# Where GpSimd's product pairs, the silu and softplus passes and y's sums stand in the order of a two-layer attention and state-space kernel

## The chip, the cores and the metric

The kernel runs on one core of one Trainium2 chip. The metric is the device time of one execution in microseconds; the time given for a kernel is the median over its runs. Shorter is better.

## What is computed

The input x has the shape (2, 256, 256, 128), f32. Two layers follow each other, each added to its own input after a group normalisation. The first is a row attention (q, k, v1, v2 and output projections of 128 channels). The second, in which the change lies, is a selective scan over the tokens of each image:

```python
xz = x @ in_proj_w.T;  xi, z = split(xz)              # 2 x 256 channels
xi = silu(depthwise_conv3x3(xi) + conv_b)              # xs
dts, Bs, Cs = split(x_proj_w @ xs)                     # 8, 16, 16 rows
delta = softplus(dt_w @ dts + dt_b)
h = exp(delta * A) * h + (delta * xs) * Bs             # per token, 256 x 16 states
y = sum_over_16_states(h * Cs) + Ds * xs
y = layernorm(y) * silu(z)
out = x + y @ out_proj_w.T
```

## The kernel before, in words

The first layer runs call by call until about 2670 us of the span; the rest is the second layer. That is cut into 128 steps (2 images x 64) of four image rows, T = 1024 tokens each. The 256 channels x 16 states of a step are 32 units of 128 partitions (32 channels x 4 states) by 1024 tokens. `unit(t)` (line 912 on) gives for unit t the step k, the half h of the channels (16 units each), the group m of four states and the quarter q of the half's channels. Four consecutive units share m, so their products sum into the same rows of y.

The order of all compute engines is written out by hand: under `tc.manual_schedule` a loop over slots t (lines 1051 to 1081) issues, once per unit, the instructions of that slot, and each engine executes its own in that order. What a slot holds for unit t:

- `drive` (line 960, instruction at 966): GpSimd multiplies delta\*x by B for a pair of units, 128 x 2048. Its buffer `hb` has room for three pairs. A pair is driven three slots ahead.
- `decay` (line 952, instruction at 956): ScalarE writes exp(delta\*A) of unit t+1 to PSUM, `da0` or `da1`, one buffer each for even and odd units.
- `scan` (978): VectorE runs the recurrence along the 1024 tokens.
- the product with C: either `product` (992), VectorE, one unit of 1024, right after its scan; or, for units in the list `POOLED`, `products` (1001), GpSimd, both units of the pair at once, two slots after the first of them. For these the scan writes to `hb` in place of PSUM. `POOLED` names the first unit of each pair; five pairs of sixteen are GpSimd's. The products lie in `yc`, which has room for four pairs.
- `add_up` (1024): eight TensorE matmul instructions (x16 in the profile) sum four units' products over the states into `y`, in PSUM, which has one buffer. They free two pairs of `yc`. `start_up` (1015) begins a new y with Ds\*xs every 16 units; `y_out` (1037) is ScalarE's copy of a finished y to SBUF, in slots 3 and 19, ahead of that slot's other pieces.
- `remember` (983): ScalarE keeps the last column of h as the next step's start.

Between these stand the pieces that prepare later steps and finish earlier ones. `project(k)` begins 72 slots ahead of step k: `turn` (658) and `normalise` (663) bring in rows, `conv` (676) is nine taps of matmuls for each half of channels and of tokens, `gate` (702) computes z, `states` (726) and `size` (744) compute B, C and delta. Their results all pass through one PSUM bank, the pool `ps_p`, so each piece waits until ScalarE has copied the one before it, one slot later (`conv_out` 687, `gate_out` 713, `states_out` 739, `size_out` 755). Three passes of ScalarE over a whole step, each between two loads of its function table, are `silu_z` (718), `silu_xs` (695) and `softplus` (763). `times` (773) forms delta\*x on GpSimd. `finish(k)` works off one row per eight slots: TensorE turns y (`turn`, 828), ScalarE sums squares (`stats`, 840), scales (`scales`, 846 and 848) and normalises (`norm`, 852), TensorE turns back (`back`, 863), VectorE multiplies by the silu of z (`gated`, 871), TensorE mixes (`mix`, 875 and 879), ScalarE copies out (`leave`, 889). Its PSUM pool `ps_f` has one bank.

Seen within a step of 32 slots, the pieces fall in four octaves of the same pattern: `turn` and three small pieces of `project` in the first four slots, then the nine taps of a conv over four slots, `back` in the second of these, `mix` in the last:

| slots | small pieces through the bank | conv taps | finishing row |
|---|---|---|---|
| 0 to 7 | states 0, 1; size at 2 | 3 to 6 | turn 0, back 4, mix 7 |
| 8 to 15 | size at 8, 9, 10 | 11 to 14 | turn 8, back 12, mix 15 |
| 16 to 23 | gate at 16, 17, 18 | 19 to 22 | turn 16, back 20, mix 23 |
| 24 to 31 | turn at 24, 25; gate at 26 | 27 to 30 | turn 24, back 28, mix 31 |

`start_up` stands in slots 5 and 21. `others` of a slot (everything but TensorE's pieces) are issued ahead of `on_pe` (TensorE's).

## Time and profile before

| | before |
|---|---|
| median of 3 runs | 16394.46 us (16359.25 to 16439.24) |
| span of the profiled run | 16364.8 us |
| mean granted TensorE clock | 0.917 |
| scan, VectorE | x4096, 2346 ns (to PSUM), 2338 ns (to SBUF) |
| product, VectorE, one unit | x2816, 1225 ns |
| pair of products, GpSimd | x640, 4531 ns |
| drive of a pair, GpSimd | x2048, 4543 ns |
| decay, ScalarE | x4096, 1122 ns |

A profile row of instruction groups names line, engine, operation, output and inputs, count, then busy time and the mean of one in ns, then the idle time of the engine just ahead of them with what ended most of it. A timeline row has start (us from the span's start), duration, engine, line and operation; in brackets stands the idle time ahead of it and what released it. Rows of consecutive like instructions are merged (x16). The answer on stretches has for each stretch its length, the busy time of PE, PEld, DVE, ACT and POOL with counts, then the granted TensorE clock as a share of full speed, the busy share of the DMA engines and GB/s. The waits view gives, for an engine's line and what it waited for, the total in us, how often, and the longest. In these rows DVE is VectorE, ACT ScalarE, POOL GpSimd, PE TensorE.

### The profile page before, as it was taken

The numbers are of one execution on the slowest core, as the hardware profiler recorded it, in microseconds if no ns is written. First come the engines' busy times: TensorE is split into PE (matmuls) and PEld (weight loads), VectorE is DVE, ScalarE is ACT, GpSimd is POOL, SyncE is SP. The second block draws the span as 40 slices with busy tenths as digits, with TensorE's granted clock in tenths as the row PEclk, the third lists the DMA queues.
The fourth block names the chain that finished last, engine by engine and source line by source line (L and its number), as shares of the span: only waits on it lengthen the run. The fifth ranks groups of instructions, "written<-read, shape, count | busy, mean of one in ns | idle before, by whom it ended". The sixth has DMA issues, their size and how long they took to land. (4 is left out here: it accounts for less than half of the span.)

```text
span 16364.8 us, 178796 instructions
## 1 busy us (share of the span) xinstructions
PE 14102.2 (86%) x59451; PEld 7209.7 (44%) x59451; DVE 14625.1 (89%) x12484; ACT 10765.1 (66%) x20003; POOL 13046.0 (80%) x3216
## 2 busy tenths in 40 slices
PE   6999997888888888888888888888888888888886
PEld 5877883333333333333333333333333333333333
DVE  7665555999999999999999999999999999999998
ACT  3555554666666666676666666666666666666665
POOL 0111114999999999999999899999999999999997
PEclk9999998899999898998999889898999898989998
DMA  4322224666666666666666666666666666666665
GB/s 184 133 88 81 90 80 144 237 230 236 234 239 231 227 237 229 233 241 232 226 238 232 227 231 231 233 230 233 239 235 235 229 234 232 233 235 230 232 237 178
DMA packets 1428913, 3452.17 MB, mean 211 GB/s; under 512 B 119784, under 2 KB 711184, under 8 KB 1407504
## 3 DMA queue, kind: packets, MB, share of 16 engines
q1 hardware_dynamic: 1427984, 3440.73, 59.7%
q8 instruction: 467, 7.65, 0.2%
q14 instruction: 462, 3.78, 0.1%
HBM read 2752.41 MB, written 687.88 MB: 210 GB/s over the span
## 5 line engine op out<-in xcount | busy, mean ns | idle before, releaser
L966 POOL TENSOR_TENSOR hb<-du_r,bb 128x2048 f32<-128x2048 f32 x2048 | 9255.6, 4543 | 555.4 <-DVE da L978 489.1
L978 DVE TENSOR_TENSOR_SCAN da<-da,state,hb 128x1024 f32<-128x1024 f32 x2816 | 6606.1, 2346 | 141.9 <-ACT da L956 139.7
L676 PE MATMUL u_ps<-xn,w_tap 128*128 128x512 f32 x9216 | 5005.0, 691 | 718.1 <-ACT sz L713 433.9
L956 ACT ACTIVATE da<-delta_r,a_neg 128x1024 f32<-128x1024 f32 x4096 | 4595.3, 1122 | 92.8 <-ACT state L983 2.2
L992 DVE TENSOR_TENSOR yc<-da,cc 128x1024 f32<-128x1024 f32 x2816 | 3449.1, 1225 | 487.1 <-PE y L1024 326.8
L676 PEld LDWEIGHTS u_ps<-xn,w_tap 128*128 128x128 f32 x9216 | 1941.9, 221 | 3379.7 <-issue 2273.1
L1001 POOL TENSOR_TENSOR yc<-hb,cc 128x2048 f32<-128x2048 f32 x640 | 2900.0, 4531 | 365.6 <-DVE hb L978 249.3
L978 DVE TENSOR_TENSOR_SCAN hb<-da,state,hb 128x1024 f32<-128x1024 f32 x1280 | 2960.0, 2338 | 114.2 <-ACT da L956 114.2
L983 ACT COPY state<-da 128x1 f32<-128x1 f32 x2816 | 454.0, 161 | 2857.2 <-DVE yc L992 2852.4
L1024 PE MATMUL y<-yc,sel 128*32 128x512 f32 x16384 | 2191.9, 654 | 18.0 <-POOL yc L1001 18.0
L435 POOL TENSOR_TENSOR x1g<-xc,bo_all 128x512 f32<-128x512 f32 x256 | 315.7, 1271 | 1843.8 <-DVE stats L484 1842.8
L828 PE MATMUL yt<-centre,ys 128*128 128x256 f32 x4096 | 1034.4, 396 | 471.1 <-ACT ob L889 471.1
L385 ACT ACTIVATE e<-s_ps,nmx 128x256 f32<-128x256 f32 x1024 | 478.6, 477 | 968.5 <-DVE nmx L376 952.4
L1024 PEld LDWEIGHTS y<-yc,sel 128*32 128x32 f32 x16384 | 451.9, 114 | 1475.6 <-issue 1221.9
L828 PEld LDWEIGHTS yt<-centre,ys 128*128 128x128 f32 x4096 | 744.2, 191 | 651.9 <-ACT ob L889 568.5
L744 PE MATMUL dt_ps<-xd,w_dt 8*128 8x512 f32 x1024 | 646.8, 715 | 322.8 <-ACT delta L755 139.7
L702 PE MATMUL z_ps<-xn,w_z 128*128 128x512 f32 x1024 | 569.6, 638 | 411.2 <-ACT sz L713 249.7
L879 PE MATMUL o_ps<-w_out,szr 128*128 128x128 f32 x4096 | 798.0, 277 | 0.0
L879 PE MATMUL o_ps<-w_out,yg 128*128 128x128 f32 x4096 | 797.3, 277 | 0.0
L889 ACT COPY ob<-o_ps 128x256 f32<-128x256 f32 x512 | 189.3, 370 | 860.8 <-PE o_ps L879 827.7
L352 DVE TENSOR_TENSOR v<-v_ps,bv_all 128x512 f32<-128x512 f32 x256 | 177.1, 692 | 593.1 <-PE v_ps L345 593.1
L879 PEld LDWEIGHTS o_ps<-w_out,yg 128*128 128x128 f32 x4096 | 668.5, 194 | 27.6
(133 smaller groups left out, 16988.4 us busy)
## 6 DMA issues: line engine op xcount, KB each, us to landing
bb<-bc_d SPq DMA_DIRECT2D x1024, 512.0 KB, 4.5
cc<-bc_d SPq DMA_DIRECT2D x1024, 512.0 KB, 4.5
delta_r<-delta_d SPq DMA_DIRECT2D x1024, 512.0 KB, 6.1
du_r<-du_d SPq DMA_DIRECT2D x1024, 512.0 KB, 5.5
sz_d<-sz SPq DMA_DIRECT2D x128, 1024.0 KB, 6.6
szr<-sz_d SPq DMA_DIRECT2D x512, 256.0 KB, 5.8
xs_d<-xs SPq DMA_DIRECT2D x128, 1024.0 KB, 6.7
xr<-xs_d SPq DMA_DIRECT2D x256, 512.0 KB, 5.3
```

What stands on the lines that cost most here:

```text
L385: nc.scalar.activation(e[:, i, :], o["s", r][:, i, :], AF.Exp, bias=o["nmx", r][:, i : i + 1], scale=SM, accum_out=o["den"][:, r, i : i + 1],)
L676: nc.tensor.matmul(o["u"], w_tap[:, h, tap, :], xn[:, i * RB + dy : i * RB + dy + RB, dx : dx + W], start=(tap == 0), stop=(tap == 8),)
L702: nc.tensor.matmul(o["z"], w_z[:, h, :], xn[:, 1 + i * RB : 1 + (i + 1) * RB, 1 : W + 1], start=True, stop=True,)
L744: nc.tensor.matmul(o["dt"], w_dt[:, h, :], o["xd"][0:DR, i * TB : (i + 1) * TB], start=True, stop=True,)
L828: nc.tensor.matmul(o["yt"][:, j, :], ys[k, h][:, t0 + j * P : t0 + (j + 1) * P], centre[:, (1 - h) * P : (1 - h) * P + DI], start=(h == 0) ...
L879: nc.tensor.matmul(o["o"][:, j, :], o[by][:, h, j * P : (j + 1) * P], w_out[:, i, h, :], start=False, stop=(j == WT - 1 and h == NH - 1 an ...
L956: nc.scalar.activation(da, spreads["delta", k, h, q], AF.Exp, scale=a_neg[:, g, m : m + 1])
L966: nc.gpsimd.tensor_tensor(hb, spreads["pair", k, h, q], repeats["bb", k, h, m].unsqueeze(1).to_broadcast([P, 2, T]), ALU.mult,)
L978: nc.vector.tensor_tensor_scan(u["h"], u["da"], u["hb"], st, ALU.mult, ALU.add)
L992: nc.vector.tensor_tensor(u["yc"], u["h"], repeats["cc", k, h, m], ALU.mult)
L1001: nc.gpsimd.tensor_tensor(yc, hb, repeats["cc", k, h, m].unsqueeze(1).to_broadcast([P, 2, T]), ALU.mult)
L1024: nc.tensor.matmul(y[q * CQ : (q + 1) * CQ, cols], sel, units[t + q]["yc"][:, cols], start=False, stop=(m == NSG - 1),)
```

## The change

Four things change, all of them in what stands where in the hand-written order; no instruction is added or taken away.

- `POOLED`: GpSimd's five pairs of products are those of units 6, 14, 22, 30, which end each eight scans, and 26; they were those of 2, 6, 10, 18 and 26.
- `silu_z`, `silu_xs` and `softplus` move up by one slot, from slots 21, 29 and 13 of a step to 20, 28 and 12: with the pairs of units 22, 30 and 14 now GpSimd's, the passes stand a slot further from those pairs' decays.
- `gated`, the product with silu of z on VectorE, moves up by one slot, from 6, 14, 22 and 30 to 5, 13, 21 and 29, ahead of those pairs' scans.
- `add_up` is always issued at the end of the slot two after its last unit, behind all TensorE pieces of that slot. Before, this held only where the second pair of the four units was GpSimd's; otherwise the sums stood a slot earlier, ahead of the slot's TensorE pieces. It was so for the groups of units 12 to 15, 20 to 23 and 28 to 31, whose sums stood in slots 17, 25 and 1 (of the next step) and now stand at the end of 18, 26 and 2.

```diff
@@ -587,7 +587,7 @@
-    POOLED = (2, 6, 10, 18, 26)
+    POOLED = (6, 14, 22, 26, 30)
@@ -790,15 +790,15 @@
-        at(base + 29, silu_z)
-        at(base + 37, silu_xs)
+        at(base + 28, silu_z)
+        at(base + 36, silu_xs)
...
-        at(base + 53, softplus)
+        at(base + 52, softplus)
@@ -899,7 +899,7 @@
             (2, scales),
             (3, norm),
             (4, back),
-            (6, gated),
+            (5, gated),
             (7, mix),
             (8, leave),
@@ -1070,13 +1070,11 @@
             for piece, args in others:
                 piece(*args)
-            if 0 <= t - 5 < end and (t - 5) % NQ == 0 and not pooled(t - 2):
-                add_up(t - 5)
             for piece, args in on_pe:
                 piece(*args)
             if 0 <= t - 5 < end and (t - 5) % NM == 0:
                 start_up(t - 5)
-            if 0 <= t - 6 < end and (t - 6) % NQ == 0 and pooled(t - 3):
+            if 0 <= t - 6 < end and (t - 6) % NQ == 0:
                 add_up(t - 6)
             if 0 <= t < end:
                 remember(t)
```

## The prediction

> **What bounds the kernel now.** First the page: engine totals and groups.

> ```profile
> PE 14102.2 (86%) x59451; PEld 7209.7 (44%) x59451; DVE 14625.1 (89%) x12484; ACT 10765.1 (66%) x20003; POOL 13046.0 (80%) x3216
> L978 DVE TENSOR_TENSOR_SCAN da<-da,state,hb 128x1024 f32<-128x1024 f32 x2816 | 6606.1, 2346 | 141.9 <-ACT da L956 139.7
> L992 DVE TENSOR_TENSOR yc<-da,cc 128x1024 f32<-128x1024 f32 x2816 | 3449.1, 1225 | 487.1 <-PE y L1024 326.8
> L1001 POOL TENSOR_TENSOR yc<-hb,cc 128x2048 f32<-128x2048 f32 x640 | 2900.0, 4531 | 365.6 <-DVE hb L978 249.3
> ```

> The state memsets (line 1056) start at 2670.9 and 9496.8 us, 64 steps apart: 106.65 us per step, 128 steps, 83% of the span. VectorE (DVE) sets the pace. In one ordinary step (unit 0 scans at 8626.47 us, the next step's at +105.75) it pauses three times; its waits between 4000 and 9000 us, and those three in the timeline:

> ```profile
> DVE yc L992 <- PE y L1024: 117.6, 94, 2.4
> DVE hb L978 <- ACT da L956: 38.3, 47, 0.8
> ```

> ```profile
> 8653.56 1.23 DVE L992 TENSOR_TENSOR yc<-da,cc 128x1024 f32<-128x1024 f32 x1 [0.96 <-PE y L1024]
> 8661.41 2.35 DVE L978 TENSOR_TENSOR_SCAN hb<-da,state,hb 128x1024 f32<-128x1024 f32 x1 [0.81 <-ACT da L956]
> 8667.02 1.23 DVE L992 TENSOR_TENSOR yc<-da,cc 128x1024 f32<-128x1024 f32 x1 [1.01 <-PE y L1024]
> ```

> They are units 8, 11 and 12 of the 32. Without them the step is 105.75 - 2.78 = 102.97 us; over the mean step DVE therefore loses 106.65 - 102.97 = 3.7 us, 471 us in 128 steps. That is all the change can win on DVE. Why is TensorE (PE) late with y's sums? The same step on PE, then its granted clock in stretches (PEclk is the third column from the end):

> ```profile
> 8660.23 1.12 PE L744 MATMUL dt_ps<-xd,w_dt 8*128 8x512 f32 x2 [0.78 <-ACT state L983]
> 8662.46 1.12 PE L744 MATMUL dt_ps<-xd,w_dt 8*128 8x512 f32 x2 [1.12 <-ACT delta L755]
> 8663.51 3.49 PE L1024 MATMUL y<-yc,sel 128*32 128x512 f32 x16
> ...
> 8683.97 1.92 PE L1024 MATMUL y<-yc,sel 128*32 128x512 f32 x16
> ...
> 8688.92 1.13 PE L702 MATMUL z_ps<-xn,w_z 128*128 128x512 f32 x2 [1.97 <-ACT sz L713]
> 8692.30 5.49 PE L676 MATMUL u_ps<-xn,w_tap 128*128 128x512 f32 x6 [2.26 <-ACT sz L713]
> ```

> ```profile
> 8660.25:8663.66 3.41, 2.29 (x8) 0.71 (x12) 2.60 (x2) 3.37 (x7) 3.41 (x2) 1.00 0.36 138
> 8663.66:8667.10 3.44, 3.44 (x17) 0.61 (x12) 2.43 (x3) 2.29 (x5) 3.44 (x2) 0.51 0.80 291
> 8687.50:8690.92 3.42, 1.13 (x2) 0.30 (x2) 3.42 (x2) 3.37 (x7) 3.42 (x2) 1.00 1.07 394
> 8690.92:8697.80 6.88, 5.50 (x8) 2.28 (x9) 6.75 (x5) 5.49 (x10) 6.80 (x3) 0.51 0.60 224
> ```

> One set of sums takes 1.92 us at full clock and 3.49 at half. Half clock follows a stretch of 3.41 us in which PE was busy 2.29 us or less, which is where it trades one PSUM bank with ScalarE (ACT) piece by piece: slots 0-3, 8-11, 16-19, 24-27. Last, ACT around slot 19, where y leaves PSUM (line 1037), and the silu pass in slot 21:

> ```profile
> 8688.30 0.57 ACT L713 COPY sz<-z_ps 128x512 f32<-128x512 f32 x1
> ...
> 8690.03 1.00 ACT L1037 COPY ys<-y 128x1024 f32<-128x1024 f32 x1
> ...
> 8696.02 1.28 ACT L718 ACT_TABLE_LOAD   x1
> 8697.31 1.91 ACT L718 ACTIVATE sz<-sz 128x2048 f32<-128x2048 f32 x1
> 8699.24 1.28 ACT L619 ACT_TABLE_LOAD   x1
> ```

> y_out waits for nothing here: its sums ran at 8683.97, ahead of the slot's piece. A pass with its two table loads occupies ACT for 4.5 us.

> [...]

> **The change, part by part.** Time runs from unit 0's scan. Unit lengths from the step above: 3.55 us with DVE's product, 2.25 without, plus 0.60 for each of four gate products.

> *The pairs.* Five before, five after; 10 x 2.25 + 22 x 3.55 + 4 x 0.60 = 103.0 either way: no DVE or POOL work is saved. What moves is where DVE runs fast. Before, units 2, 3, 6, 7 and 10 shorten the stretch in which PE has the dt pieces, nine taps and y's start: from scan 3 (9.4) to product 8's turn (26.1) are 16.7 us. After, 10.65 to 28.85: 18.2. PE's stretch from the first tap to the end of the sums was 13.38 to 26.98, 13.6 us, and begins about 4.6 us after scan 3: 28.85. The wait at 8 shrinks from 1 us to some 0.35 (nought if warm, 1.4 if PE comes late). The waits at 11 and 12 go: no pair lies at 10. POOL keeps up (a drive takes 4.5 us, a pair of products 4.5, a delta product 2.35, and a drive needs the buffer of three pairs before): drive 18 starts at 46.6 behind scan 13; with the first delta product after it, pair 14's products run from 53.4 to 57.9, the second to 60.3, drives 20, 22, 24, 26 to 78.4, products 22 from scan 23's end at 79.3 to 83.8, drives 28 and 30 to 92.9, products 26 to 97.4, drive 32 to 102.0. Scans 20, 28 and 32 are due at 67.0, 90.9 and 103.0: no wait for POOL, with 1.0 us to spare at the least.

> *Gate products up a slot.* Four of 0.67 us, as many as before. They ask for the transposes back at 21.3, 47.7, 74.3 and about 101; these end at 20.0, 45.1, 72.6 to 75.2, and about 100. The third can be late by 0.9, but scan 22 is then waiting for ACT anyway (below). Cost 0.

> *Softplus (slot 12) and silu of xs (28).* 4.5 us of ACT each. Softplus ends at 46.55, decay 14 at 47.9, scan 14 is at 48.3: hidden behind scans 12 and 13 and their products. Silu of xs likewise hides behind units 28 and 29. Cost 0.

> *The sums behind the pieces.* Sets that were ahead (slots 1, 17, 25) now stand after the piece of slots 2, 18, 26. This adds waits. Slot 18: gate piece starts when ACT has copied the previous one, scan 18 (59.9) + 2.42 = 62.3. Without the early sums PE is busy from 54.7 to 57.5, then only from 59.3 to 60.35: any 3.41 us window ending between 58.5 and 61.9 leaves it at half clock. So piece 2.0 (twice 1.0, to 64.35) and sums 1.9 to 3.7, taken as 2.85 since a busy window may end in them: they end at about 67.2 (65.3 if both are warm, 68.0 at worst). y_out, formerly free at scan 19 + 1.5 = 64.9, waits until then. Behind it in ACT's queue stand y_out, norm, gate copy (2.1 together, as traced): 69.35, then decay 21 to 70.6 (scan 21 at 70.55: 0.1 lost).

> *Silu of z in slot 20* comes next in that queue: 70.6 + 4.5 = 75.1, remember and decay 22 to 76.4. Scan 22 is due at 74.75: 1.65 us lost (0 to 2.6).

> *Octave 24 to 31.* With 22 and 26 pooled DVE is fast where PE does taps, y's start, mix, and the turns. The taps start at 69.4; nine taps of 0.89, transposes 0.44, y's start 1.72, sums 1.85 and 1.7 for one cold window end at 83.1; product 24 asks at 83.4: mean loss 0.2. Mix (2.3) ends at 85.4, leave 85.7, conv copy and xn copy 86.75, decay 26 88.05, stats 89.05, normalise 89.75, decay 27 91.05, against a scan due at 90.35: 0.7, the old wait at unit 11 (0.81) again. Slot 26: the second normalise (scales 0.4, normalise 0.65 after decay 27) lets the gate piece start at 92.15; PE had only two turns of 0.55 since 87.6, so it is cold: piece 2.0, sums 2.8 (1.9 to 3.7): 97.0. Product 28 asks at 93.3 + 2.45 = 95.75: 1.3 (0.3 to 2.1).

> Sum: 0.35 + 0.1 + 1.65 + 0.2 + 0.7 + 1.3 = 4.3 us per step in place of 3.7: +0.6 x 128 = +77 us. At the very end the last pair is POOL's 4.53 us instead of a DVE product: +4. 16394 + 81 = 16475 us.

> **Rivals.** *Forecast (0.46): the three waits move, two of them onto cold sums; slightly slower,* 16475. For it: a cold 3.49 us set is already in the trace exactly where one stands behind such a piece. *Faster (0.26): PE stays warm* behind the pieces, so y_out and product 28 don't wait: 4.3 - 1.65 - 1.3 = 1.3 us, -2.4 x 128 = -307: about 16090. For it: pairs now lie mostly where ACT and PE don't trade a bank. Against it: 1.05 us of work in a 3.4 us window is less than what went cold before. *Slower by much (0.13): lateness is handed on:* 22 at 2.6, 27 at 0.75, 28 at 2.0, 8 at 1.4, in all 6.75, +3.05 x 128 = +390: about 16785. For it: the chain mix, leave, turn, stats has no slack after unit 24. *No change (0.15):* waits at 22 and 28 just replace those at 8 and 12, 16395.

> **How the numbers follow.** The loss per step has its centre at 4.3, only just past the 0.5% bound (82 us, 0.64 us per step): of the forecast about 0.33 lies above it, 0.08 within and 0.05 below. Slower 0.33 + 0.13 = 0.46; same 0.08 + 0.14 = 0.22; faster 0.26 + 0.05 + 0.01 = 0.32. The range takes in the forecast's cold bounds (losses 2.5 to 6.4) and part of the faster case: 16170 to 16740.

> **What would show it.** Right: DVE waits for ACT at unit 22 of about 1.65 us and for PE at unit 28 of about 1.3; none at 11 or 12; y_out with a wait of about 2 us on PE; sums in slots 18 and 26 at 2.9 to 3.5 us; mean granted clock in the steps near 0.89 instead of 0.92. Wrong: sums of 1.92 us there with few DVE waits (faster), a DVE wait on POOL (pairs or drives late, which I put at zero), or waits at unit 8 above 1 us (slower by much).

## The result and the profile after

The changed kernel takes 16291.85 us (median of 4 runs, 16285.8 to 16300.5) against 16388.42 us before (median of 4; one run more than in the table above): ratio 0.9938, 95% interval 0.9913 to 0.9964. It is 0.6% faster, where 0.5% slower was forecast.

Engine totals and the groups that answer to those shown of before, from the page of the changed kernel:

```profile
PE 13879.5 (85%) x59451; PEld 7046.9 (43%) x59451; DVE 14642.8 (90%) x12484; ACT 10842.9 (67%) x20003; POOL 13035.7 (80%) x3216
L978 DVE TENSOR_TENSOR_SCAN da<-da,state,hb 128x1024 f32<-128x1024 f32 x2816 | 6607.2, 2346 | 163.1 <-ACT da L956 160.2
L992 DVE TENSOR_TENSOR yc<-da,cc 128x1024 f32<-128x1024 f32 x2816 | 3449.1, 1225 | 287.3 <-PE y L1024 113.8
L1001 POOL TENSOR_TENSOR yc<-hb,cc 128x2048 f32<-128x2048 f32 x640 | 2908.7, 4545 | 527.6 <-ACT state L983 493.0
```

The work is the same to the instruction. The idle time ahead of VectorE's products has gone from 487 to 287 us. The state memsets start at 2675.1 and 9471.4 us, so a step takes 106.19 us on average where it took 106.65. Both means take in one long step at the change of images, 121.27 us before and 120.88 after; without it the steps average 106.44 and 105.86 us. So some 0.2 of the 3.7 us that the prediction counted as the old loss per step is this one step.

In the first image most steps take about 105.81 us. VectorE's waits between 4000 and 9000 us (line waited at, total, times, longest), and the same waits in one such step, which starts at 7550.13 us:

```profile
DVE hb L978 <- ACT state L983: 80.0, 82, 1.7
DVE yc L992 <- PE y L1024: 14.8, 16, 2.2
DVE hb L978 <- ACT da L956: 8.5, 39, 0.2
```

```profile
7626.58 4.59 DVE L978 TENSOR_TENSOR_SCAN hb<-da,state,hb 128x1024 f32<-128x1024 f32 x2 [1.44 <-ACT state L983]
7640.94 2.35 DVE L978 TENSOR_TENSOR_SCAN hb<-da,state,hb 128x1024 f32<-128x1024 f32 x1 [0.22 <-ACT da L956]
7651.43 4.59 DVE L978 TENSOR_TENSOR_SCAN hb<-da,state,hb 128x1024 f32<-128x1024 f32 x2 [0.42 <-ACT state L983]
```

These are units 22, 27 and 30: in such a step the waits for TensorE at units 8 and 12 are gone, and the large wait is now for ScalarE. The second image looks different. From about 10300 to 14600 us steps of 106.10 and 105.53 us alternate. The waits between 10000 and 15000 us, then those of one long step (from 11906.32 us: units 21, 22, 28) and of the short one after it (from 12012.42 us: units 8, 12, 28):

```profile
DVE yc L992 <- PE y L1024: 69.8, 90, 1.4
DVE hb L978 <- ACT state L983: 41.8, 27, 1.7
DVE da L978 <- ACT da L956: 18.7, 22, 0.9
```

```profile
11977.86 2.36 DVE L978 TENSOR_TENSOR_SCAN da<-da,state,hb 128x1024 f32<-128x1024 f32 x1 [0.85 <-ACT da L956]
11983.78 4.59 DVE L978 TENSOR_TENSOR_SCAN hb<-da,state,hb 128x1024 f32<-128x1024 f32 x2 [1.71 <-ACT state L983]
12002.65 1.23 DVE L992 TENSOR_TENSOR yc<-da,cc 128x1024 f32<-128x1024 f32 x1 [0.44 <-PE y L1024]
...
12042.01 1.23 DVE L992 TENSOR_TENSOR yc<-da,cc 128x1024 f32<-128x1024 f32 x1 [0.86 <-PE y L1024]
12056.59 1.23 DVE L992 TENSOR_TENSOR yc<-da,cc 128x1024 f32<-128x1024 f32 x1 [0.41 <-PE y L1024]
12108.18 1.23 DVE L992 TENSOR_TENSOR yc<-da,cc 128x1024 f32<-128x1024 f32 x1 [1.42 <-PE y L1024]
```

So product 28 waits for TensorE in all of these, and the wait at unit 22 is in every second step only. Back to the step from 7550.13 us: ScalarE's timeline shows the cause of its wait at unit 22, y_out waiting for the late sums, with the silu pass right behind:

```profile
7617.17 1.01 ACT L1037 COPY ys<-y 128x1024 f32<-128x1024 f32 x1 [2.11 <-PE y L1024]
...
7619.50 1.12 ACT L956 ACTIVATE da<-delta_r,a_neg 128x1024 f32<-128x1024 f32 x1
7620.64 1.28 ACT L718 ACT_TABLE_LOAD   x1
7621.94 1.91 ACT L718 ACTIVATE sz<-sz 128x2048 f32<-128x2048 f32 x1
7623.87 1.28 ACT L619 ACT_TABLE_LOAD   x1
...
7625.35 1.12 ACT L956 ACTIVATE da<-delta_r,a_neg 128x1024 f32<-128x1024 f32 x1
```

In the same step, TensorE's timeline at slots 18 and 26, and the granted clock (third column from the end) in stretches of about 3.41 us:

```profile
7612.45 1.95 PE L702 MATMUL z_ps<-xn,w_z 128*128 128x512 f32 x2 [2.09 <-ACT sz L713]
7614.33 2.74 PE L1024 MATMUL y<-yc,sel 128*32 128x512 f32 x16
...
7642.08 1.13 PE L702 MATMUL z_ps<-xn,w_z 128*128 128x512 f32 x2 [1.67 <-ACT xn L663]
7643.14 1.92 PE L1024 MATMUL y<-yc,sel 128*32 128x512 f32 x16
```

```profile
7585.40:7588.87 3.47, 2.36 (x8) 0.69 (x12) 3.37 (x3) 3.41 (x7) 3.47 (x2) 0.98 0.53 171
7588.87:7592.28 3.41, 3.41 (x17) 0.56 (x10) 3.38 (x3) 2.56 (x6) 3.41 (x2) 0.52 0.95 294
...
7636.66:7640.07 3.41, 2.10 (x14) 1.66 (x13) 3.26 (x3) 3.35 (x10) 3.41 (x1) 1.00 0.63 192
7640.07:7643.48 3.41, 1.74 (x10) 0.56 (x11) 3.19 (x3) 3.38 (x8) 3.41 (x2) 1.00 0.43 141
```

Slot 18's sums ran partly at half clock, as forecast (2.74 us). Slot 26's ran at full clock (1.92), though TensorE was busy for only 2.10 and 1.74 us in the two stretches up to them; yet 2.36 us in the stretch of slots 9 and 10 were followed by half clock (granted 0.52, and the sums of slot 10 took 3.61 us). And 105.81 us are 31 times 3.413 us, as 106.10 + 105.53 = 211.63 us are 62 times; 3.413 us is the spacing of the granted clock's changes, measured below. These two facts are what the experiments are about.

### The profile page after: what moved, and what is told of

Read it like the earlier page. It is cut to its first block, busy times and chain, and to the rows that moved or that the text cites. A ratio compares the mean times of both kernels' runs of the same rounds, so it can differ in the third digit from the quotient of the medians.

```text
span 16298.5 us, 178168 instructions
## 1 busy us (share of the span) xinstructions
PE 13879.5 (85%) x59451; PEld 7046.9 (43%) x59451; DVE 14642.8 (90%) x12484; ACT 10842.9 (67%) x20003; POOL 13035.7 (80%) x3216
## 5 line engine op out<-in xcount | busy, mean ns | idle before, releaser
L978 DVE TENSOR_TENSOR_SCAN da<-da,state,hb 128x1024 f32<-128x1024 f32 x2816 | 6607.2, 2346 | 163.1 <-ACT da L956 160.2
L676 PE MATMUL u_ps<-xn,w_tap 128*128 128x512 f32 x9216 | 4481.8, 629 | 617.0 <-ACT state L983 607.5
L956 ACT ACTIVATE da<-delta_r,a_neg 128x1024 f32<-128x1024 f32 x4096 | 4588.5, 1120 | 91.8 <-ACT state L983 0.4
L992 DVE TENSOR_TENSOR yc<-da,cc 128x1024 f32<-128x1024 f32 x2816 | 3449.1, 1225 | 287.3 <-PE y L1024 113.8
L1001 POOL TENSOR_TENSOR yc<-hb,cc 128x2048 f32<-128x2048 f32 x640 | 2908.7, 4545 | 527.6 <-ACT state L983 493.0
L978 DVE TENSOR_TENSOR_SCAN hb<-da,state,hb 128x1024 f32<-128x1024 f32 x1280 | 2941.9, 2336 | 199.1 <-ACT state L983 166.4
L676 PEld LDWEIGHTS u_ps<-xn,w_tap 128*128 128x128 f32 x9216 | 1762.1, 201 | 3108.4 <-issue 2110.6
L1024 PE MATMUL y<-yc,sel 128*32 128x512 f32 x16384 | 2409.3, 712 | 16.6 <-POOL yc L1001 16.6
L983 ACT COPY state<-da 128x1 f32<-128x1 f32 x2816 | 458.2, 163 | 1266.7 <-DVE yc L992 1262.4
L1024 PEld LDWEIGHTS y<-yc,sel 128*32 128x32 f32 x16384 | 477.4, 121 | 1743.3 <-issue 1518.6
L702 PE MATMUL z_ps<-xn,w_z 128*128 128x512 f32 x1024 | 691.8, 763 | 628.2 <-ACT sz L713 389.6
L983 ACT COPY state<-hb 128x1 f32<-128x1 f32 x1280 | 247.0, 193 | 1262.2 <-DVE hb L978 1262.2
L744 PE MATMUL dt_ps<-xd,w_dt 8*128 8x512 f32 x1024 | 611.7, 678 | 345.2 <-ACT state L983 193.7
```

Source lines behind the costliest of these rows:

```text
L676: nc.tensor.matmul(o["u"], w_tap[:, h, tap, :], xn[:, i * RB + dy : i * RB + dy + RB, dx : dx + W], start=(tap == 0), stop=(tap == 8),)
L702: nc.tensor.matmul(o["z"], w_z[:, h, :], xn[:, 1 + i * RB : 1 + (i + 1) * RB, 1 : W + 1], start=True, stop=True,)
L744: nc.tensor.matmul(o["dt"], w_dt[:, h, :], o["xd"][0:DR, i * TB : (i + 1) * TB], start=True, stop=True,)
L956: nc.scalar.activation(da, spreads["delta", k, h, q], AF.Exp, scale=a_neg[:, g, m : m + 1])
L978: nc.vector.tensor_tensor_scan(u["h"], u["da"], u["hb"], st, ALU.mult, ALU.add)
L983: nc.scalar.copy(st, units[t]["h"][:, T - 1 : T])
```

## The experiments

Two theories were set against each other. SUM: each wait of VectorE adds to the step (the prediction's way of counting). LOCK: a step is drawn to a whole number of TensorE's clock windows, because a window's place in the step decides how late the sums are. The windows are read from the traces: in the second layer every one of the 1058 falls and rises of the granted clock in before, and of the 931 in after, lies on one grid of 3.4133 us, to 0.011 us, through steps of different length. A window is the stretch between two points of that grid, and 105.81 / 31 = 3.413 agrees. Mean step below is the distance of the two state memsets over 64 and so takes in the change of images. The last column has the step, or the repeating group of steps, that is most frequent among all 127. Ratios are to the kernel before on the same chip.

| kernel | us, median | ratio, 95% interval | mean step | most frequent step or group |
|---|---|---|---|---|
| before | 16388 | | 106.65 | 105.74 |
| after | 16292 | 0.9938 [0.9913, 0.9964] | 106.19 | 105.81; 105.53 and 106.10 in turn |
| before_late | 17134 | 1.0472 [1.0455, 1.0489] | 112.68 | 112.64 |
| after_passes | 16688 | 1.0201 [1.0186, 1.0216] | 109.28 | 109.44 |
| after_gates | 16339 | 0.9987 [0.9980, 0.9995] | 106.37 | 105.81 |
| after_sum17 | 16169 | 0.9883 [0.9868, 0.9898] | 105.22 | 104.40, 103.45, 106.18 in turn |
| after_pad | 16383 | 1.0011 [1.0005, 1.0018] | 106.99 | none |
| after_sum17_25 | 16281 | 0.9958 [0.9944, 0.9972] | 105.95 | 105.81 |
| after_dt128 | 16284 | 0.9959 [0.9944, 0.9974] | 106.13 | 105.79 to 105.81 |
| before_dt128 | 16255 | 0.9941 [0.9926, 0.9956] | 106.00 | 105.81 |
| after_both | 16274 | 0.9952 [0.9937, 0.9967] | 105.99 | 105.81 |
| both_warm | 16187 | 0.9917 [0.9902, 0.9932] | 105.29 | eight in turn, 104.15 to 106.05 |
| both_warmlead | 16122 | 0.9879 [0.9862, 0.9895] | 104.87 | 103.81 |
| both_lead | 15963 | 0.9779 [0.9764, 0.9793] | 103.55 | 102.99 |

The groups are whole numbers of windows too: 104.40 + 103.45 + 106.18 = 314.03 us are 92 windows, and the eight steps of both_warm, 839.68 us, are 246. So what LOCK says of one step holds for a group of two, three or eight as well, which neither the prediction nor the expectations below had in mind.

### The parts of the change

The sums alone, added to the kernel before:

```diff
-            if 0 <= t - 5 < end and (t - 5) % NQ == 0 and not pooled(t - 2):
-                add_up(t - 5)
-            if 0 <= t - 6 < end and (t - 6) % NQ == 0 and pooled(t - 3):
+            if 0 <= t - 6 < end and (t - 6) % NQ == 0:
```

> The kernel before with the sums alone changed: all of them at the end of the slot two after their last unit, pairs, passes and gate products as before. y_out in slot 19 must wait for cold sums as in the changed kernel, to about 67.2 us of a step; decay 21 then ends at 70.6, and scan 21 is due at 68.1 because pair 18 is short: 2.4 us of wait at unit 21 on top of the waits at 8, 11, 12. SUM: 106.65 + 2.4 gives about 109 us per step, 16690 us. LOCK: 32 windows, 109.2 us per step, 16720 us. If the late sums cost nothing (my forecast's mechanism is wrong): 16390 us.

It takes 17134 us, slower than either theory said. Three of the waits of one step (from 5024.0 us), at units 5, 8 and 21, in its VectorE timeline:

```profile
5041.05 2.36 DVE L978 TENSOR_TENSOR_SCAN da<-da,state,hb 128x1024 f32<-128x1024 f32 x1 [1.72 <-ACT da L956]
...
5053.71 1.23 DVE L992 TENSOR_TENSOR yc<-da,cc 128x1024 f32<-128x1024 f32 x1 [1.69 <-PE y L1024]
...
5098.95 2.36 DVE L978 TENSOR_TENSOR_SCAN da<-da,state,hb 128x1024 f32<-128x1024 f32 x1 [2.21 <-ACT da L956]
```

The wait of 2.2 us at unit 21 is there as worked out (2.4), and a second y_out, in slot 3, does the same to unit 5 (1.72), which I had not counted; product 20 waits 1.04 us for the sums besides. The late sums are the costly part of the change: 4.7%. The step is 112.64 us, 33 windows and not 32, and the same in step after step. LOCK alone doesn't tell which whole number.

The pairs can't be moved without the sums: early sums of units 0 to 3 and 16 to 19 would stand ahead of the start of their y. So the next kernel has pairs and sums, with passes and gate products in their former slots:

```diff
-        at(base + 28, silu_z)
-        at(base + 36, silu_xs)
+        at(base + 29, silu_z)
+        at(base + 37, silu_xs)
-        at(base + 52, softplus)
+        at(base + 53, softplus)
-            (5, gated),
+            (6, gated),
```

> The changed kernel with the silu and softplus passes and the gate products back in their former slots; the pairs and the sums as in the changed kernel. Each pass then stands between the two decays of a GpSimd pair: decays 15, 23 and 31 are late by about 1.4, 1.1 and 1.4 us, in place of the waits at 22 (1.44) and 30 (0.42). SUM: the losses go from 2.8 to about 4.8 us per step, about 16530 us. LOCK: steps can't be 105.81 us any more and are drawn towards 109.2 (16720 us) or run uneven between. If the passes' slots don't matter: 16292 us.

The waits lie where they were expected: units 15, 23 and 31 wait for decays 0.86, 0.82 and 0.86 us per step, less than expected. The time is nearer LOCK's figure than SUM's, but the steps run between 106.8 and 110.3 us and are held at 109.2 for a few at a time only. With the sums late, moving the pairs brings the time from 17134 to 16688 us, about 2.6%, and the passes and gate products bring another 2.6%. In the waits view of this kernel the decays lead:

```profile
DVE hb L978 <- ACT da L956: 145.8, 225, 0.9
DVE yc L992 <- PE y L1024: 112.8, 110, 2.2
```

The gate products alone, put back in the changed kernel (`(6, gated)` for `(5, gated)`):

> The changed kernel with the gate products alone back in slots 6, 14, 22 and 30, between the two scans of a GpSimd pair; passes, pairs and sums as changed. If the 2.6% between after_passes and the changed kernel are the passes' alone: the gate product moves from ahead of scan 22 to behind it, scan 22 asks 0.6 us sooner and waits 0.6 us longer, nothing else changes, the steps stay at 105.81 us, 16280 to 16310 us. If the gate products' slot is part of the gain: above 16350 us.

16339 us, in between the two expectations, and by the ratios 0.5% above the changed kernel. The steps are 105.81 us in one stretch, held by waits at 8, 12, 22 and 28 (0.85, 0.41, 0.56, 1.14 us), and 105.9 to 109 in others. So most of the 2.6% belongs to the passes, and with the gate products in their former slots the mean step is longer, 106.37 for 106.19 us.

### y_out's wait and the lock

Only the sums of units 12 to 15 are put back ahead of slot 17's piece:

```diff
+            if 0 <= t - 5 < end and (t - 5) % NU in (12,):
+                add_up(t - 5)
             for piece, args in on_pe:
                 piece(*args)
...
-            if 0 <= t - 6 < end and (t - 6) % NQ == 0:
+            if 0 <= t - 6 < end and (t - 6) % NQ == 0 and (t - 6) % NU not in (12,):
```

> The changed kernel with the sums of units 12 to 15 alone put back ahead of slot 17's TensorE piece, so that y_out in slot 19 finds y finished. If the wait at unit 22 is caused by y_out waiting for sums behind the gate piece, it vanishes, and so does y_out's wait in slot 19. SUM: steps fall from 105.8 to about 104.4 us, -1.4 x 128 = -180 us, about 16110 us. LOCK: without that wait nothing holds a step at 105.81; either other waits (units 8, 27, 28) grow until it is 105.81 again, 16290 us, or steps get uneven, between 103.5 and 105.5 us, about 16050 to 16250 us.

The wait at unit 22 is gone, so its cause is shown. But the mean step falls by 1.0 us and not by 1.4. Single steps take from 103.4 to 106.9 us, three quarters of them in the group of three that is 92 windows long, so the kernel has found another hold, at 104.7 us per step. The waits view says what comes instead:

```profile
DVE yc L992 <- PE y L1024: 54.1, 55, 2.2
DVE hb L978 <- ACT da L956: 23.8, 71, 0.8
DVE hb L978 <- ACT state L983: 9.2, 26, 0.4
```

The first row is for the most part unit 28, 0.93 us per step on average and 2.19 in the worst steps: the wait on cold sums in slot 26 that the prediction put at 1.3 us. It comes in those steps in which the clock window falls badly. In the changed kernel the steps of 105.81 us are not among them, and those of 105.53 and 106.10 us are (1.42 and 0.44).

One more instruction per step on VectorE:

```diff
+        def pad():
+            nc.vector.bn_stats(s1.tile([P, 6], F32, name="pad"), centre)
...
+        at(base + 50, pad)
```

> The changed kernel with one more VectorE instruction per step, a reading of 384 columns after product 10, which should take about 0.45 us (estimate: a 128-column one takes 0.21 us in the trace of before); it computes nothing that is used. Theory LOCK (a step of the changed kernel is drawn to 31 of TensorE's clock windows of 3.413 us, 105.81 us, and the wait at unit 22 gives way): steps stay at 105.81 us, the wait at unit 22 falls from 1.44 to about 1.0 us, time 16275 to 16310 us. Theory SUM (every wait and instruction of VectorE adds up): steps grow by 0.45 us, 128 x 0.45 = 58 us, about 16350 us.

Both theories missed. The instruction takes 0.54 us (the estimate's base was low too: the 128-column readings of before take 0.28 us in the trace, not 0.21); the mean step grows by 0.80. Some steps, 7 of 127, are still within 0.03 us of 105.81, absorbing all of it, but the hold doesn't last: other steps take 106.3 to 109.2, with waits of 1.45 and 2.19 us at unit 28. If 105.81 us holds a step, it does so only within narrow limits.

Both sets of sums that stand behind a gate piece, in slots 18 and 26, are now put early, `in (12, 20)` for `in (12,)`:

> The changed kernel with two sets of sums ahead of their slot's TensorE piece: units 12 to 15 in slot 17 (as in after_sum17, whose steps averaged 105.2 us) and units 20 to 23 in slot 25. In after_sum17 what remained was a wait at unit 28 (0.93 us per step on average, 2.2 us in the steps in which slot 26's sums ran at half clock) and at 26 and 27 (0.5). COLD SUMS (the sums behind slot 26's gate piece cost 0 to 2.2 us according to where the clock window falls): the wait at 28 vanishes, steps come to about 104.2 us, about 16040 us. If the wait at 28 has another cause it stays: 16170 us.

The wait at 28 vanishes, as it should. But the time is 16281 us: the steps are back at 105.81 us, now made of quite other losses (0.60 at the gate product of slot 5, 1.28 at unit 8, 0.41 at 12, 0.41 at 30). Here adding up waits is off by 240 us and LOCK holds.

### What lets the clock fall

The delta matmuls run on 8 rows (8\*128 in the profile, where the gate pieces and taps have 128\*128). In the kernel before, the ten sets of sums right behind them between 4400 and 5420 us took 3.22 to 3.64 us. Two readings are set against each other: ROWS, that matmuls on 8 rows do less to keep the clock up than matmuls on 128 rows of the same busy time; and TIME, that busy time alone counts. The delta matmuls are widened with zero rows, in the changed kernel and in the one before:

```diff
-    w_dt = const.tile([DR, NH, P], F32, name="w_dt")
+    w_dt = const.tile([P, NH, P], F32, name="w_dt")
+    nc.vector.memset(w_dt, 0.0)
...
-                o["xd"][0:DR, i * TB : (i + 1) * TB],
+                o["xd"][:, i * TB : (i + 1) * TB],
```

> The changed kernel with the delta matmuls (dt_ps) over all 128 rows of the array, the added rows zero; same result, same columns. ROWS [...]: slot 10's sums run at full clock, 1.9 us in place of 3.6, the mean clock rises by about 0.016; the steps leave the place where they were held, so the time may fall or rise, 16150 to 16400 us. TIME (only the busy share of a window counts, 2.29 of 3.41 us being too little): slot 10's sums stay at 3.6 us and the time at 16290 us.

> The kernel before with the delta matmuls over all 128 rows, as in after_dt128. ROWS: slot 10's sums take 1.9 us, the wait at unit 12 (1.0 to 2.1 us) goes, the waits at 8 and 11 stay: steps of about 104.8 us, 106.65 - 104.8 = 1.8, about 16150 us. TIME: nothing changes, 16360 us.

TensorE's timeline of before_dt128 in slots 8 to 10, then its VectorE waits in the same step (from 5416.02 us):

```profile
5448.97 1.02 PE L747 MATMUL dt_ps<-xd,w_dt 128*128 128x512 f32 x2
5450.77 1.12 PE L747 MATMUL dt_ps<-xd,w_dt 128*128 128x512 f32 x2 [0.78 <-ACT state L986]
5452.99 1.13 PE L747 MATMUL dt_ps<-xd,w_dt 128*128 128x512 f32 x2 [1.10 <-ACT delta L758]
5454.05 1.92 PE L1027 MATMUL y<-yc,sel 128*32 128x512 f32 x16
```

```profile
5444.30 1.23 DVE L995 TENSOR_TENSOR yc<-da,cc 128x1024 f32<-128x1024 f32 x1 [2.15 <-PE y L1027]
5451.95 2.35 DVE L981 TENSOR_TENSOR_SCAN hb<-da,state,hb 128x1024 f32<-128x1024 f32 x1 [0.62 <-ACT da L959]
```

ROWS is right: with the same busy times and gaps (0.78 and 1.1 us), slot 10's sums take 1.92 us instead of 3.2 to 3.6, in both kernels (1.92 to 1.93 in nine steps of each between 4400 and 5420 us). The wait at unit 12 is gone. And still SUM fails: in the usual step of before_dt128 the wait at unit 8 has grown from about 1.0 to 2.15 us, and the step is 105.81 us. What was saved in one place was lost in another. The kernel is as fast as the changed one all the same (0.9941): most steps take 105.81 us or stand in a group of four that averages it (124 windows), they no longer slip to 106.8 us and more, and without the change of images they average 105.63 us where those of before average 106.44. In the changed kernel the edit gains nothing that is clear of noise (0.9959 for 0.9938).

Both edits together:

> The sums as in after_sum17_25 and the delta matmuls over 128 rows as in after_dt128. ROWS and COLD SUMS: no sums at half clock stand ahead of a waiting product; only the waits at 26 and 27 (0 to 0.6 us) remain, steps of about 103.5 us, about 15950 us. Neither: 16170 us.

The expected 15950 us don't come: 16274, and 105.81 us per step again, from waits at 8, 24, 26, 27 and 30 (0.89, 0.65, 0.45, 0.21, 0.41). Half clock now falls on the taps that follow ScalarE's slow slots 3, 19 and 27 (16 to 19, 67 to 74 and 94 to 98 us of a step).

### Out of the lock

Two ways out: keep TensorE busy, or make the half clock harmless by starting the taps sooner. The first issues the gate and delta pieces of four slots twice:

```diff
+            for _ in range(1 if (h, i) == (0, 1) else 2):
+                nc.tensor.matmul(o["z"], ..., start=True, stop=True)
...
+            for _ in range(2 if (h, i) == (0, 0) else 1):
+                nc.tensor.matmul(o["dt"], ..., start=True, stop=True)
```

> after_both with the gate pieces of slots 17, 18 and 26 and the delta piece of slot 2 issued twice (the second matmul writes the same values over the first, 1.05 us of TensorE each), to keep TensorE busy where it waits for ScalarE. after_both's steps are 105.81 us with half clock from 16 to 19, 67 to 74 and 94 to 98 us of a step. LOCK BY THE CLOCK WINDOW: with fewer or no half-clock stretches the waits at 8, 24, 26 and 27 (0.92, 0.66, 0.45, 0.21 us) shrink and nothing holds the step at 105.81: 103.4 to 104.5 us, 15960 to 16110 us. If 105.81 us has another cause than the clock windows, or more work on TensorE only costs: 16270 us or more.

The mean clock rises from 0.937 to 0.962 and no single step length dominates: 104.2 to 106.1 us, mostly in the group of eight. But the doubled pieces come late themselves, with waits at 5, 8 and 30 (0.37, 0.65, 0.84 us), so 16187 us is short of what was expected. The second lets the copy that frees the bank go ahead of norm and y_out on ScalarE:

```diff
-            at(base + t + 1, gate_out, h, i)
+            at(base + t + 1, gate_out, h, i, lead=(h == i))
-            at(base + t + 1, size_out, h, i)
+            at(base + t + 1, size_out, h, i, lead=(h == i))
...
-            if 0 <= t - 7 < end and unit(t - 7)[2:] == (NSG - 1, 0):
-                y_out(t - 7)
             others, on_pe = slots.pop(t, ((), ()))
             for piece, args in others:
                 piece(*args)
+            if 0 <= t - 7 < end and unit(t - 7)[2:] == (NSG - 1, 0):
+                y_out(t - 7)
```

(`lead` puts the piece first in its slot.)

> after_both with ScalarE's order changed in slots 3, 11, 19 and 27: the copy that lets the next conv start (gate_out or size_out) goes ahead of norm and y_out, so taps start some 0.7 to 1.7 us earlier. LOCK: lateness of the taps is what the waits at 8, 24, 26 and 27 give back; they shrink and the step either leaves 105.81 us downwards, to 103.4 to 105 us (15960 to 16160 us), or finds another phase with the same 105.81 us (16270 us). SUM: 1.5 us less wait per step, 16080 us.

15963 us, 2.2% below the kernel before and, by the two ratios (0.9779 / 0.9938), 1.6% below the changed one. The waits view of VectorE from 4000 to 9000 us, all of it:

```profile
DVE hb L982 <- ACT state L987: 7.9, 19, 0.8
DVE yc L996 <- issue: 2.2, 5, 0.5
DVE yc L996 <- DVE da L982: 1.4, 3, 0.5
DVE da L982 <- ACT da L960: 0.2, 1, 0.2
```

Some steps have no wait at all and take 102.98 to 103.03 us, which is what was worked out for the step without waits (102.97). Its mean clock is 0.941, so half clock still occurs; nothing on VectorE's path ends on it any more.

> both_warm and both_lead together. LOCK BY THE CLOCK WINDOW: full clock nearly throughout and taps that start early leave only the wait at unit 30 (0.41 us): steps of 103.4 us, about 15960 us, and clock 0.97 or more. If the waits don't depend on the clock: as both_lead.

With both, ScalarE's copy of slot 27 waits for the doubled gate piece of slot 26 (0.98 us in the step from 3926.3 us), silu of xs comes later, and unit 30 waits 1.29 us per step: 16122 us. Of the two, only the early taps are wanted. What they would bring to the changed kernel alone, without the two edits of after_both, was not tried.

## Why the prediction was wrong, point by point

**The bound.** Right. VectorE sets the pace, 102.97 us without waits, and both_lead comes to within 0.6 us of it.

**The change's free edits.** The moved pairs cost no wait on GpSimd, as worked out. The gate product of slot 21 is some 0.1 us late, within the 0.9 allowed and hidden by the wait at 22, as said. Silu of xs, put at 0, costs 0.42 at unit 30 in steps of 105.81 us and 0.20 on average.

**The wait at unit 22.** Right in mechanism and size: y_out was to start at 67.2 us of the step and starts at 67.04; scan 22 was to start at 76.4 and starts at 76.45; the wait was to be 1.65 and is 1.44, in a step of 105.81 us; over all steps it averages 1.10. after_sum17 confirms its cause.

**The old waits.** Those at 8, 11 and 12 were to shrink to 0.35 or go. Unit 11 no longer waits. Units 8 and 12 wait for nothing in steps of 105.81 us, and 0.85 and 0.41 in those of 105.53.

**The step that failed** is, in slot 26, "PE had only two turns of 0.55 since 87.6, so it is cold: piece 2.0, sums 2.8", 1.3 us in every step, added to the 1.65 us at unit 22. The terms per step, as forecast, as the mean over 119 steps of the changed kernel (without the first and last four and the change of images), and in its three usual kinds of step:

| wait at unit | forecast | mean | steps of 105.81 | of 106.10 | of 105.53 |
|---|---|---|---|---|---|
| 8 | 0.35 | 0.25 | 0 | 0 | 0.85 |
| 12 | 0 | 0.12 | 0 | 0 | 0.41 |
| 21 | 0.1 | 0.21 | 0 | 0.85 | 0 |
| 22 | 1.65 | 1.10 | 1.45 | 1.71 | 0 |
| 24 | 0.2 | 0 | 0 | 0 | 0 |
| 27 | 0.7 | 0.10 | 0.21 | 0 | 0 |
| 28 | 1.3 | 0.54 | 0 | 0.44 | 1.42 |
| 30 | 0 | 0.20 | 0.42 | 0 | 0 |

In only 3 of the 119 steps do units 22 and 28 both wait more than 1 us: where one set of sums costs its full wait, the other costs little or nothing. In steps of 105.81 us slot 26's piece and sums run at full clock. Over all steps its sums do average what was forecast (2.73 us for 2.8, as slot 18's average 2.72 for 2.85), but its piece takes 1.44 and not 2.0, and the sums end at 94.9, 96.3 and 95.7 us in the three kinds of step and not at 97.0. The mean granted clock, which was to fall to 0.89 in the steps, rose from 0.917 to 0.935 over the run.

Two readings behind this were wrong. First, the rule. I read from the kernel before that 2.29 us of work in a window let the clock fall, and took it for a matter of busy time; those were delta matmuls on 8 rows, which count for less (the sums behind them take 3.2 to 3.6 us, and 1.92 once they are widened in before_dt128 and after_dt128). In the changed kernel 1.74 us of work on 128 rows in a window kept the clock up (1.00 granted). Second, the alignment. I took all places of the window as equally likely and averaged, place by place. But each kind of step has one place of the window, for slots 18 and 26 together, and the steps repeat few places: one where slot 26 costs nought, and a pair where it costs 1.42 and 0.44.

**The sum.** The forecast's terms make 4.3 us. Measured from the step without waits, 102.97 us, the 119 steps lose 2.92 us, and those of 105.81 us lose 2.84; the waits in the table make 2.52 of the 2.92, and the rest, in pauses of about 0.1 us and less, was not followed up. That the losses can be forecast one by one and added is what fell: six kernels with different waits have the same usual step, 105.79 to 105.81 us, and a seventh has 112.64 = 33 x 3.413.

**What the gain is.** The ordinary step is hardly shorter than before: 105.81, alone or as the mean of the pair, against 105.74. The kernel before, however, doesn't hold it. Its steps start 0.07 us earlier against the window each time (105.81 - 105.74), with waits at 8 and 12 that change in opposite directions (0.83 and 1.15, then 0.99 and 0.94), so that the step's length stays the same and nothing pulls it back. After some steps it slips, and the next ones take 106.8 to 108.5 us; for some steps it then is held at a longer length, 106.77 and 108.26 in turn, 63 windows in two steps. In the changed kernel a step that starts 0.12 us later against the window is 0.05 us shorter (105.76 against 105.81), which draws it back. The return is plainer in after_both: a step of 105.99 us is followed by steps of 105.73, 105.77, 105.79, 105.80 and 105.81. Fewer slips make 106.65 into 106.19: 0.46 x 128 = 59 us of the 66 us between the two profiled spans. That the restoring slope comes from the sums of slot 18, whose end moves with the window's, is argued from this and not tried by itself. Why a kernel settles on one step, a pair or a longer group, and when it changes from one to another, stays open.

The level of work that keeps the clock up can be told more closely from all windows of the second layer. In the kernel before, among windows at full clock without delta matmuls, the clock fell after up to 1.64 us of TensorE work (busy time in the trace, 274 windows) and stayed up from 1.61 us on (2582 windows); in after the two overlap between 1.39 and 1.69 us of the 3.41 (333 and 2679 windows).

## What to carry to other kernels

Where a loop's path passes through TensorE work whose clock falls in every round, don't add up waits: the round, or a group of two, three or more rounds, may settle on a whole number of clock windows, as here on 31 of 3.413 us, and an edit that removes a wait may gain nothing until the path no longer ends on half-clock work (here 16281 us in after_sum17_25 for 16292 in the changed kernel, but 15963 in both_lead). Take the length of every round of the whole trace first, as one stretch can hide another pattern, and divide the repeating ones by the spacing of the clock's changes in that trace; if that gives a whole number, look for what makes the chain late (here: ScalarE doing norm and a 1 us copy ahead of the copy that TensorE waits for) and not for the largest wait. In the steps of 105.81 us here, a wait in the trace said where the slack came out, not what would be saved.
